# A factorization-machine layer on one core: P7's bank read in halves by two engines, a planner fed with traced durations, held-back loads and adding DMAs for X1, X2, X4

## The chip, the core and the metric

The kernel runs on one core of a Trainium2 chip. The metric is the device time in microseconds from launch to end, as the median of several runs. The profile used here is that of one execution.

The core has a matrix engine (PE; its weight loads are listed as PEld), a vector engine (DVE), a scalar engine (ACT), a general engine (POOL) and a queue engine that only starts DMAs (SP). ACT and POOL start DMAs too. PE writes its results into the banks of PSUM, 128 partitions of 512 fp32 values each; DVE and ACT read them there.

## The reference

```python
# x: (1024, 512), weight: (64, 512, 512) = (e, f, m), lin_w: (512, 512), lin_b: (512,)
out_lin = x @ lin_w.T + lin_b
xv = jnp.einsum('bf,efm->bem', x, weight)
zp = jnp.einsum('bf,efm->bem', jnp.square(x), jnp.square(weight))
interaction = 0.5 * jnp.sum(jnp.square(xv) - zp, axis=1)
return out_lin + interaction
```

All of it is fp32. The large part is `xv`: 1024 x 512 times 512 x 32768, squared and summed over the 64 embeddings. The sum over e of `zp` is one product of the squared x with the sum over e of the squared weights.

## The kernel before

**Products by Strassen's scheme.** Each product is cut into 2 x 2 quadrants and done with seven block products instead of eight (the variant of Winograd): P1 to P7 with left operands X1 to X7, which are quadrants or sums of quadrants of x, and right operands w11, w12, w21, w22 or T, which is a running sum of them. The columns of the weights come in 32 blocks (`h`, from 0 to 31), and each block runs the seven products in the order 5, 1, 6, 2, 3, 7, 4 (product 5 of the next block runs ahead of product 4 of this one). Each product has two halves of 256 batch rows, and each half uses one pair of PSUM banks, `bank_0` to `bank_3` in turn. A pair is one tile of shape [128, 2, 512]; `(bank, 0)` and `(bank, 1)` are its halves, one bank each.

**Operands in three pieces.** To use the fast fp32r matmul at fp32 accuracy, an operand is split into pieces H (rounded), L (the rest) and K (a small correction that pairs the two). `split` makes the pieces of a weight block: ACT copies H and a first L, then POOL, or an adding DMA issued by POOL (`dma_add`), completes L, and POOL makes K. `x_pieces` makes those of X1 to X7 once: ACT makes H, DVE makes L and K. A product half runs a "front" (H and L, 4 matmuls for each half of the pair), a scaling by DVE or ACT in place, and later a "back" (K, 2 matmuls for each half). In block 0 the products 1, 2 and 4 are plain fp32 matmuls without pieces (`PLAIN`).

**After a product.** For P2, P3, P4 and P7 `finish` lets ACT square the pair into `sq`, and DVE sums groups of 16 into `acc`. For P7 DVE also subtracts p5 from the pair, into `w`, which P4 of the same block adds. A pair can be written again, four halves later, when its readers are done: the pair of a half of P7 is next written by the same half of P4.

**Ends.** Ahead of the blocks stands the linear part, seven levels of plain fp32 matmuls (`one_level`, line 494 with `by_k`, line 507 without), whose operands R5, R6, R7, R3 and column sums `lt` are made by DVE, and whose results L11 to L22 go to DRAM. `f1` to `f4` are the four pairs there. Level 1 writes f1, ACT copies f1 to f2, level 2 adds into f1, and level 6 adds into f2. At the end the same scheme runs once more for `zp`, with the sums `acc` and the linear part added in.

**The order of the work** is written out ahead by a planner (`Plan`). Every operation is given with its engine's duration and what it reads and writes. PE's order is fixed by keys. From PE's order the planner works out for each operation the latest start (`deadlines`); then it plays the engines forward (`forward`), each taking the ready operation with the earliest latest start, repeats this 60 times with changed latest starts and keeps the order with the earliest end. `HOP` is the time from one engine's end to another's start, `AHEAD` how long before its latest start SP may issue a load. The planner fixes only the order on each engine; on the chip each instruction waits for its operands. DMA issues stand in the queue of the engine that issues them, and a waiting one holds back what is behind it.

Of the kernel before, what the change touches and what calls it, by code (L numbers as in the profile page):

```python
# [22 lines left out]

PLAIN = (1, 2, 4)
# [9 lines left out]
PE, DVE, ACT, POOL, SP = "PE", "DVE", "ACT", "POOL", "SP"  # L34
# [3 lines left out]
class Plan:  # L38
    HOP = 0.3
    OWN = 0.05  # L40
    AHEAD = 50.0
# [3 lines left out]
    YIELD = 0.0  # L45

# [27 lines left out]
    def deadlines(self, chain):  # L74
# [11 lines left out]
        while stack:  # L86
            o = stack.pop()
            latest = t if o.latest is None else o.latest
            cost = min(o.costs.values()) + o.move + o.land + self.HOP
# [50 lines left out]
    def forward(self, chain):  # L140
# [6 lines left out]
        done, late, nxt, wire, held = [], 0.0, 0, [9.0], None  # L147
# [5 lines left out]
        def ready(o, e=None):  # L153
            at = self.HOP
            for d in o.deps:
                own = ops[d].engine == e and not ops[d].move
                at = max(
                    at, ops[d].end + (self.OWN * (e != PE) if own else self.HOP * (e != NONE))
                )
            return at  # L160

        def ends(e, o, at):
            free[e], o.end, running[e] = at, at + o.land, o
# [3 lines left out]
            for t in (at, o.end, o.end + self.OWN, o.end + self.HOP):  # L167
# [7 lines left out]
        def pick(e, now):  # L175
# [23 lines left out]
        while len(done) < len(ops):  # L199
            now = heapq.heappop(times)  # L200
            moved = True
            while moved:
                moved = False
                for e in pending:
# [9 lines left out]
                    if e == PE:  # L214
                        nxt += 1
                        late = max(late, now - o.latest)
                    cost = o.costs[e]
                    o.start, o.engine = now, e
                    tensor = e == POOL and not o.move
                    if e == DVE and o.both and free[POOL] > now + 0.05 and not running[POOL].move:  # L220
                        held, free[e], o.end = o, float("inf"), float("inf")
                    elif tensor and held is not None and held.latest < o.latest + self.YIELD:
                        ends(DVE, held, now + held.costs[DVE])
                        o.after, held = held, None
                        ends(e, o, o.after.end + self.HOP + cost)
# [15 lines left out]
def kernel(  # L241
# [7 lines left out]
):  # L249

# [90 lines left out]
    def act(o, i, func, reads, writes, size=1024, scale=1.0, bias=0.0):  # L341
# [3 lines left out]
        plan.add({ACT: 0.14 + 0.92 * size / 1024}, emit, reads, writes)  # L345

    def stt(o, i, scalar, j, op, reads, writes, size=512, both=False, cost=None):
# [3 lines left out]
        plan.add({DVE: cost or 0.14 + 1.08 * size / 1024}, emit, reads, writes, both=both)  # L351

    def dve(o, a, b, sub, reads, writes, size=512, both=False):
# [3 lines left out]
        plan.add({DVE: 0.14 + 1.08 * size / 1024}, emit, reads, writes, both=both)  # L357

    def pool(o, a, b, sub, reads, writes, size=1024):
# [3 lines left out]
        plan.add({POOL: 0.15 + 2.35 * size / 1024}, emit, reads, writes)  # L363

    def reduce(o, i, reads, writes):
        plan.add(
            {DVE: 1.21},
# [6 lines left out]
    def dma(o, i, reads, writes, move=1.75, on=(SP,)):  # L374
        plan.add(dict.fromkeys(on, 0.45), lambda e: queues[e].dma_start(o, i), reads, writes,
                 land=2.0, move=move)

    def dma_add(o, i, reads, writes, move=2.75):
        plan.add(
            {POOL: 0.95}, lambda _: nc.gpsimd.dma_start(o, i, accum_op=ALU.add),  # L380
            tuple(reads) + tuple(writes), writes, land=2.5, move=move,
        )
# [20 lines left out]
    def load_x(n, k, lo, hi, at):  # L403
        r, q = quads[n]
        half = H // 2
        nc.sync.dma_start(
            buf[n][:, k, lo * half:hi * half],
            x_src[:, q * KH + k, r * H + lo * half:r * H + hi * half],
        )
        for u in range(lo, hi):  # L410
            landing((n, k, u), at)
# [9 lines left out]
    load_x("A11", 0, 0, 1, 3.5)  # L421
    load_lw(nc.scalar, [0], 0, 3.5)
    load_x("A11", 0, 1, 2, 3.9)
    load_lw(nc.scalar, [1], 0, 5.2)
    load_x("A11", 1, 0, 2, 5.0)
    load_lw(nc.scalar, [2, 3], 0, 7.2)
    load_x("A12", 0, 0, 2, 6.4)
    load_x("A12", 1, 0, 2, 7.4)
    load_lw(nc.sync, [0, 1], 1, 8.4)
    load_lw(nc.sync, [2, 3], 1, 9.2)  # L430
    for at, (n, k) in enumerate((("A22", 0), ("A22", 1), ("A21", 0), ("A21", 1))):
        load_x(n, k, 0, 2, 10.0 + 0.8 * at)
    nc.scalar.dma_start(bias[:], lin_b)
    landing("bias", 9.5)
    nc.scalar.preload_act_table(AF.Square)

    def a_parts(*names):
        return tuple((n, k, u) for n in names if n in quads for k in range(KH) for u in range(2)) + tuple(
# [46 lines left out]
    def one_level(p, rhs, left, bank, first, key, by_k=False):  # L485
# [3 lines left out]
        if by_k:  # L489
            for at, (u, k) in enumerate(steps):  # L490
                for half in range(2):
                    def emit(_, u=u, k=k, half=half):
                        cols = slice(half * H // 2, (half + 1) * H // 2)
                        nc.tensor.matmul(  # L494
                            buf[bank[u]][:, cols], b[:, k, ts(u, P)], a[:, k, cols],
                            start=first and k == 0 and half == 0, stop=k == KH - 1,
                            skip_group_check=True,
                        )

                    names = (a_names[2 * k + half],) + (b_names[k],)  # L500
                    plan.add({PE: WHOLE / 2}, emit, names + (bank[u],), (bank[u],),
                             key=key + 0.1 * at + 0.05 * half)
# [416 lines left out]
```

## Time and profile before

| | |
|---|---|
| Median of 3 runs | 1300.92 us (1297.79 to 1301.03) |
| Profiled execution: whole time | 1299.58 us |
| Profiled execution: span, first to last instruction | 1297.6 us |
| PE busy | 1280.1 us (99%) |
| DVE, ACT, POOL busy | 1086.7, 1011.9, 1095.3 us |
| Granted PE clock | 0.999 |
| DMA | 200.25 MB, mean 154 GB/s |

In the lines below, each instruction or group stands as line, engine, operation, output <- input, and shape. In a timeline the first number is the start and the second the duration in us, `x8` the number of records merged into the line, and in square brackets stands how long the engine had been idle before and what released it. A plain fp32 matmul has two records. In the list of groups the numbers after the bar are the busy time in us, the mean duration in ns, and the idle time just before, with its releasers. In the list of waits the numbers are us in total, times, and longest. In the list of DMAs the last number is the median time in us from issue to landing.

### The profile page before, as it was taken

To read this page: it belongs to the slowest core of one execution; us is meant where nothing else is said; L and a number is where in the kernel's file an instruction comes from. 1 tells how busy PE (TensorE), PEld (TensorE's weight loads), DVE (VectorE), ACT (ScalarE), POOL (GpSimd) and SP (SyncE) were. 2 spreads that over 40 slices of the span, in tenths; PEclk is the share of its full clock that TensorE was granted. 3 is DMA by queue.
4 is the path that set the end of the run, shared out by engine and by line. 5 is a ranking of instruction groups with operands and counts; after the bars stand their busy time and mean duration, and the time that the engine had idled before them with its cause. 6 is when DMAs were issued, how large, how long until landed. Compare 5 with 4: busy or idle time off the path is not lost.

```text
span 1297.6 us, 15705 instructions
## 1 busy us (share of the span) xinstructions
PE 1280.1 (99%) x5484; PEld 1026.0 (79%) x5484; DVE 1086.7 (84%) x954; ACT 1011.9 (78%) x1071; POOL 1095.3 (84%) x590
## 2 busy tenths in 40 slices
PE   8999999999999999999999999999999999999997
PEld 4668888888888888888888888888888888888873
DVE  4699888888888888888888888888888889888884
ACT  5568788788777888877888887788888788888872
POOL 3659898898888899889889888888988888998891
PEclk9999999999999999999999999999999999999999
DMA  6366676757667666677766666767667676766866
GB/s 226 97 164 160 155 170 150 158 129 154 163 155 167 142 152 145 149 163 164 162 147 143 153 151 161 167 145 161 133 148 168 147 162 152 169 131 144 184 130 150
DMA packets 75998, 200.25 MB, mean 154 GB/s; under 512 B 23824, under 2 KB 25104, under 8 KB 75920
## 3 DMA queue, kind: packets, MB, share of 16 engines
q0 software_dynamic: 28512, 101.72, 44.0%
q1 hardware_dynamic: 45552, 94.91, 22.6%
q10 hardware_dynamic: 1856, 2.62, 0.6%
q8 instruction: 43, 0.70, 0.2%
q14 instruction: 35, 0.29, 0.1%
HBM read 158.34 MB, written 6.29 MB: 127 GB/s over the span
## 4 chain that ended last, share of the span: by engine, by line
PE 92%; DMA 3%; DVE 2%; ACT 1%; issue 1%; POOL 1%; SPq 0%; DVEq 0%; ACTq 0%; POOLq 0%
PE bank L678 89%; PE bank L507 3%; DMA T<-weight 1%; DMA w<-weight 1%; DMA w<-xT 0%; PE bank L494 0%; DVE w L355 0%; POOL pL L361 0%; ACT sq L343 0%; ACT wsq L343 0%; POOL pK L361 0%; ACT pL L343 0%; DVE bank L355 0%; ACT bank L343 0%; DVE bank L349 0%
## 5 line engine op out<-in xcount | busy, mean ns | idle before, releaser
L361 POOL TENSOR_TENSOR pK<-pH,pL 128x1024 fp32r<-128x1024 f32 x221 | 560.1, 2554 | 19.8 <-PE bank L678 10.8
L343 ACT ACTIVATE sq<-bank 128x1024 f32<-128x1024 f32 x256 | 261.5, 1022 | 112.8 <-DVE w L355 52.2
L368 DVE TENSOR_REDUCE acc<-sq 128x16 f32<-128x1024 f32 x256 | 306.9, 1211 | 10.7 <-ACT sq L343 10.7
L361 POOL TENSOR_TENSOR pL<-w,pL 128x1024 fp32r<-128x1024 f32 x95 | 240.3, 2530 | 13.8 <-ACT pL L343 11.8
L361 POOL TENSOR_TENSOR pL<-T,pL 128x1024 fp32r<-128x1024 f32 x64 | 155.0, 2422 | 97.2 <-ACT pL L343 95.7
L349 DVE SCALAR_TENSOR_TENSOR bank<-bank,w 128x1024 f32<-128x1024 f32 x190 | 233.0, 1226 | 3.4 <-PE bank L678 3.4
L355 DVE TENSOR_TENSOR w<-bank,p 128x1024 f32<-128x1024 f32 x128 | 156.7, 1224 | 54.6 <-PE bank L678 52.4
L349 DVE SCALAR_TENSOR_TENSOR bank<-bank,p 128x1024 f32<-128x1024 f32 x126 | 154.4, 1226 | 44.9 <-ACT p L343 35.9
L343 ACT ACTIVATE pL<-T 128x1024 fp32r<-128x1024 f32 x95 | 100.9, 1062 | 83.5 <-issue 44.2
L343 ACT ACTIVATE pL<-w 128x1024 fp32r<-128x1024 f32 x126 | 133.8, 1063 | 36.0 <-issue 29.6
L368 DVE TENSOR_REDUCE w_sum<-wsq 128x16 f32<-128x1024 f32 x128 | 155.2, 1213 | 7.9 <-ACT wsq L343 7.2
L343 ACT ACTIVATE wsq<-w 128x1024 f32<-128x1024 f32 x128 | 134.7, 1052 | 2.7 <-DVE w_sum L368 2.6
L343 ACT ACTIVATE p<-bank 128x1024 f32<-128x1024 f32 x128 | 130.1, 1018 | 8.4 <-PE bank L678 6.9
L343 ACT ACTIVATE pH<-w 128x1024 fp32r<-128x1024 f32 x126 | 133.0, 1055 | 0.0
L712 DVE TENSOR_SCALAR bank<-bank 128x1024 f32<-128x1024 f32 x62 | 76.4, 1232 | 54.8 <-PE bank L678 54.7
L343 ACT ACTIVATE pH<-T 128x1024 fp32r<-128x1024 f32 x95 | 100.0, 1052 | 0.0
L380 POOL DMA_DIRECT2D T<-weight x93 | 99.4, 1069 | 0.0
L678 PE MATMUL bank<-pH,X3H 128*128 128x512 f32 x256 | 78.9, 389 | 1.0 <-DVE w L355 1.0
L678 PE MATMUL bank<-pH,X7H 128*128 128x512 f32 x256 | 79.2, 390 | 0.4 <-ACT sq L343 0.3
L678 PE MATMUL bank<-pH,X5H 128*128 128x512 f32 x256 | 79.4, 391 | 0.0
L678 PE MATMUL bank<-pH,X2H 128*128 128x512 f32 x248 | 76.5, 389 | 2.7 <-ACT pH L343 2.7
L678 PE MATMUL bank<-pL,X7L 128*128 128x512 f32 x256 | 78.9, 389 | 0.0
(116 smaller groups left out, 2550.1 us busy)
## 6 DMA issues: line engine op xcount, KB each, us to landing
w<-weight SPq DMA_DIRECT2D x128, 512.0 KB, 5.6
T<-weight POOLq DMA_DIRECT2D x93, 512.0 KB, 7.4
T<-weight SPq DMA_DIRECT2D x32, 512.0 KB, 3.6
pL<-T POOLq DMA_DIRECT2D x31, 512.0 KB, 6.1
pL<-w POOLq DMA_DIRECT2D x31, 512.0 KB, 5.2
w<-weight POOLq DMA_DIRECT2D x31, 512.0 KB, 5.3
accd<-turned SPq DMA_DIRECT2D x64, 32.0 KB, 5.0
p<-lind SPq DMA_DIRECT2D x4, 512.0 KB, 4.7
```

Source lines behind the costliest of these rows:

```text
L343: nc.scalar.activation(o, i, func, bias=bias, scale=scale)
L349: return nc.vector.scalar_tensor_tensor(o, i, scalar, j, ALU.mult, op)
L355: return (nc.vector.tensor_sub if sub else nc.vector.tensor_add)(o, a, b)
L361: return (nc.gpsimd.tensor_sub if sub else nc.gpsimd.tensor_add)(o, a, b)
L368: lambda _: nc.vector.tensor_reduce(o, i.rearrange("p a (m e) -> p a m e", e=E), axis=AX.X, op=ALU.add),
L380: {POOL: 0.95}, lambda _: nc.gpsimd.dma_start(o, i, accum_op=ALU.add),
L507: nc.tensor.matmul(buf[bank[u]], b[:, k, ts(u, P)], a[:, k, :], start=first and k == 0, stop=k == KH - 1, skip_group_check=True,)
L678: nc.tensor.matmul(buf[bank, j], buf[x][:, k, ts(2 * half + j, P)], buf[w][:, k, :], start=first and k == 0, stop=k == KH - 1, skip_group_ ...
L712: plan.add({DVE: 1.2}, lambda _, o=o: nc.vector.tensor_scalar(o, o, 1 + U, None, ALU.mult), names, names)
```

## The change

What it does, part by part:

- **P7's pair in halves.** ACT squares half 0 while DVE subtracts from half 1; then DVE takes half 0 and ACT half 1.
- **X1, X2, X4.** L and K are made by ACT copies and adding DMAs (two each) instead of by DVE.
- **Sums of weights in block 0** are adding DMAs from DRAM instead of POOL sums (`MORE`).
- **The linear part.** The first loads are 256 KB each, the weights' on ACT's queue, those of x on SP's. The first two levels use whole-width matmuls. Level 2 writes a pair of its own, DVE adds it to L11, and the copy f1 to f2 goes; level 6 adds into f1. The last part does the same: f1 is added to the output early, and two ACT copies go.
- **The planner** gets new durations, a tail for each engine, `HOP` 0.06, `AHEAD` 20, and `SOON`: POOL's DMAs are not issued more than 25 us before their latest start. A DMA that the planner held back gets a wait for the PE operation that was running then.
- The scale S moves from the pieces of X into the squares, and U into the reads of plain products. These cost no instruction.

The diff, cut to these parts:

```diff
+MORE = True
+X_SPLIT = {5: DVE, 6: DVE, 3: DVE, 7: DVE, 1: "DMA", 2: "DMA", 4: "DMA"}
+FIRST = dict.fromkeys(range(1, 8), "POOL")
...
-    HOP = 0.3
-    OWN = 0.05
-    AHEAD = 50.0
+    HOP = 0.06
+    TAIL = {"PE": 0.17, "DVE": 0.09, "ACT": 0.11, "POOL": 0.05, "SP": 0.0, "": 0.0}
+    AHEAD = 20.0
+    SOON = 25.0
...
+                if e == POOL and o.move and o.latest - self.SOON > now + 1e-6:
+                    heapq.heappush(times, o.latest - self.SOON)
+                    continue
...
+                    if o.move and o.emit and mark and now - ready(o, e) > 0.3 and now > free[e] + 0.1:
+                        o.after = mark
...
-        plan.add({ACT: 0.14 + 0.92 * size / 1024}, emit, reads, writes)
+        plan.add({ACT: 0.06 + 0.89 * size / 1024}, emit, reads, writes)
-        plan.add({DVE: 0.14 + 1.08 * size / 1024}, emit, reads, writes, both=both)
+        plan.add({DVE: 0.06 + 1.08 * size / 1024}, emit, reads, writes, both=both)
-        plan.add({POOL: 0.15 + 2.35 * size / 1024}, emit, reads, writes)
+        plan.add({POOL: 0.1 + 2.24 * size / 1024}, emit, reads, writes)
-    def dma_add(o, i, reads, writes, move=2.75):
+    def dma_add(o, i, reads, writes, move=3.1, land=1.8):
         plan.add(
-            {POOL: 0.95}, lambda _: nc.gpsimd.dma_start(o, i, accum_op=ALU.add),
+            {POOL: 0.62}, lambda _: nc.gpsimd.dma_start(o, i, accum_op=ALU.add),
...
-    load_x("A11", 0, 0, 1, 3.5)
-    load_lw(nc.scalar, [0], 0, 3.5)
-    load_x("A11", 0, 1, 2, 3.9)
-    load_lw(nc.scalar, [1], 0, 5.2)
-    load_x("A11", 1, 0, 2, 5.0)
-    load_lw(nc.scalar, [2, 3], 0, 7.2)
-    load_x("A12", 0, 0, 2, 6.4)
-    load_x("A12", 1, 0, 2, 7.4)
-    load_lw(nc.sync, [0, 1], 1, 8.4)
-    load_lw(nc.sync, [2, 3], 1, 9.2)
+    load_x("A11", 0, 3.9)
+    load_lw(nc.scalar, [0, 1], 0, 3.9)
+    load_x("A11", 1, 5.2)
+    load_lw(nc.scalar, [2, 3], 0, 5.6)
+    load_x("A12", 0, 7.4)
+    load_lw(nc.scalar, [0, 1], 1, 7.8)
+    load_x("A12", 1, 8.2)
+    load_lw(nc.scalar, [2, 3], 1, 8.8)
...
     def x_pieces(i):
         n, (h, l, k) = OPERAND[i], (f"X{i}{z}" for z in "HLK")
-        act(buf[h], buf[n], AF.Copy, a_parts(n), (h,), scale=S * TRIM)
-        stt(buf[l], buf[n], S, f32(h), ALU.subtract, a_parts(n) + (h,), (l,), 1024, True)
-        stt(buf[k], f32(h), -U, f32(l), ALU.add, (h, l), (k,), 1024, True)
+        parts = a_parts(n)
+        act(buf[h], buf[n], AF.Copy, parts, (h,), scale=TRIM)
+        if X_SPLIT[i] == "DMA":
+            act(buf[l], buf[n], AF.Copy, parts, (l,), scale=-TRIM)
+            dma_add(f32(l), buf[n], parts, (l,))
+            act(buf[k], buf[n], AF.Copy, parts, (k,), scale=-U * TRIM)
+            dma_add(f32(k), f32(l), (l,), (k,))
+        else:
+            dve(buf[l], buf[n], f32(h), True, parts + (h,), (l,), 1024, True)
+            stt(buf[k], f32(h), -U, f32(l), ALU.add, (h, l), (k,), 1024, True)
...
     one_level(1, lin_rhs, lhs, f1, True, -1000, True)
-    for u in range(2):
-        act(buf[f2[u]], buf[f1[u]], AF.Copy, (f1[u],), (f2[u],), 512)
-    one_level(2, lin_rhs, lhs, f1, False, -990, True)
     lin_copy("L11", f1, 0, 1.0)
+    one_level(2, lin_rhs, lhs, f2, True, -990, True)
+    lin_add("L11", f2, False)
     lin_store("L11", 0, 0)
...
-    one_level(6, lin_rhs, lhs, f2, False, -960)
+    one_level(6, lin_rhs, lhs, f1, False, -960)
...
-        if h:
+        if h or MORE:
             dma_add(buf[o], src(h, q), (), (o,))
...
     def finish(h, p, half, bank):
         row, col = {2: (0, 0), 3: (0, 1), 4: (1, 0), 7: (1, 1)}[p]
         sq, a = square(), acc_name[h // NCB]
-        act(buf[sq], buf[bank], AF.Square, both_of(bank), (sq,))
         m, b = (2 * col + h % NCB) * MI, row * NJ + 2 * half
+        if p == 7:
+            n, p5 = value["w", h, half], value["p5", h, half]
+            used((sq, 0), sq)
+            used((sq, 1), sq)
+
+            def square_of(k):
+                act(buf[sq][:, k], buf[bank, k], AF.Square, ((bank, k),), ((sq, k), (bank, k)),
+                    512, scale=S)
+
+            def rest_of(k):
+                dve(buf[n, k], buf[bank, k], buf[p5, k], True, (p5, (bank, k)),
+                    ((n, k), (bank, k)))
+
+            square_of(0)
+            rest_of(1)
+            rest_of(0)
+            square_of(1)
+            used(sq, (sq, 0), (sq, 1))
+        else:
+            act(buf[sq], buf[bank], AF.Square, both_of(bank), (sq,), scale=S)
         reduce(buf[a][:, b:b + 2, m:m + MI], buf[sq], (sq,), ((a, b // 2, m),))
...
-            if p == 7:
-                n, p5 = value["w", h, half], value["p5", h, half]
-                dve(buf[n], o, buf[p5], True, (p5, *names), (n,), 1024)
...
     one_level(1, right, left, f1, True, key)
     for u in range(2):
-        act(buf[f2[u]], buf[f1[u]], AF.Copy, (f1[u],), (f2[u],), 512, -1.0)
+        into(o_name[0, 0], f1, False, u)
...
-    one_level(2, right, left, f1, False, key + 20)
+    one_level(2, right, left, f2, True, key + 20)
```

More of the change, by code (lines that the diff above doesn't have):

```diff
@@ L22 @@
 TRIM = 1.0 - 2.0 ** -13
+PE, DVE, ACT, POOL, SP = "PE", "DVE", "ACT", "POOL", "SP"
 PLAIN = (1, 2, 4)
@@ L224, in forward @@
                         o.after, held = held, None
[L225 removed]
+                        ends(e, o, free[DVE] + 0.15 + cost)
                     elif tensor and held is None and free[DVE] > now and running[DVE].both:
@@ L490, in one_level, with emit @@
             for at, (u, k) in enumerate(steps):
[L491 to L502, printed above, removed]
+                def emit(_, u=u, k=k):
+                    return nc.tensor.matmul(
+                        buf[bank[u]], b[:, k, ts(u, P)], a[:, k, :], start=first and k == 0,
+                        stop=k == KH - 1, skip_group_check=True,
+                    )
+                plan.add({PE: WHOLE}, emit, (a_names[k], b_names[k], bank[u]), (bank[u],),
+                         key=key + 0.1 * at)
             return
@@ L885 @@
                 ),
-                reason="the port that VectorE and GpSimd share",
+                reason="the order of transfers, or of two engines at the port that they share",
             )
```

105 lines of the change are left out of this document (52 added, 53 removed).

## The prediction

> **What bounds the kernel now.** I read the profile's page first, then the busy time by stages, then who PE waited for, and last the timelines of the places where it waited.
>
> ```profile
> span 1297.6 us, 15705 instructions
> PE 1280.1 (99%) x5484; PEld 1026.0 (79%) x5484; DVE 1086.7 (84%) x954; ACT 1011.9 (78%) x1071; POOL 1095.3 (84%) x590
> ```
>
> PE is busy for 1280.1 of 1297.6 us, and the change keeps every matmul (32 half-width ones become 16 whole ones), so only the 17.5 us in which PE stands still can be won. The view by stages says where they lie; its first columns are the stretch, its length and PE's busy time in it.
>
> ```profile
> 0.00:33.10 33.10, 28.59 (x76) 14.91 (x77) 15.35 (x14) 18.09 (x23) 11.90 (x10) 1.00 0.68 222
> 33.10:95.00 61.90, 58.16 (x211) 39.21 (x210) 50.71 (x43) 37.46 (x39) 38.03 (x20) 1.00 0.46 130
> 95.00:150.00 55.00, 54.67 (x240) 44.40 (x239) 47.77 (x42) 42.37 (x46) 48.82 (x26) 1.00 0.67 152
> 150.00:1250.00 1100.00, 1099.88 (x4846) 905.93 (x4845) 943.55 (x824) 896.26 (x945) 978.12 (x521) 1.00 0.69 154
> 1250.00:1291.50 41.50, 38.76 (x118) 21.56 (x116) 26.86 (x30) 17.73 (x23) 18.48 (x16) 1.00 0.67 140
> 1291.50:1297.60 6.10, 0.01 (x1) 0.00 (x0) 2.49 (x4) 0.00 (x0) 0.00 (x0) 0.81 0.46 172
> ```
>
> Idle by stage: 4.51 us in the linear part, 3.74 in the first products, 0.33, then 0.12 in the 1100 us of the steady loop, 2.74 in the last level and 6.10 of adding and storing after the last matmul. The loop has nothing to give; it can only lose. The whole run of this profile took 1299.58 us, 1.98 more than its span and 1.34 below the median of 1300.92; I sum against 1299.58. About 0.3%, 3.9 us, is what can be told from no change: below 1297.0 is faster, above 1304.8 slower.
>
> **The linear part.**
>
> ```profile
> 4.33 2.25 PE L494 MATMUL bank<-w,p 128*128 128x256 f32 x8
> 8.18 1.53 PE L494 MATMUL bank<-w,p 128*128 128x256 f32 x6 [1.60 <-DMA w<-xT]
> 10.38 0.70 PE L494 MATMUL bank<-w,p 128*128 128x256 f32 x2 [0.67 <-ACT bank L343]
> 11.75 3.29 PE L494 MATMUL bank<-w,p 128*128 128x256 f32 x14 [0.67 <-ACT bank L343]
> 15.82 0.70 PE L494 MATMUL bank<-w,p 128*128 128x256 f32 x2 [0.78 <-ACT wsq L343]
> 16.36 3.60 PE L507 MATMUL bank<-w,p 128*128 128x512 f32 x8
> 19.79 7.03 PE L507 MATMUL bank<-sq,p 128*128 128x512 f32 x16
> 33.12 1.02 PE L678 MATMUL bank<-pH,X5H 128*128 128x512 f32 x2
> 9.75 0.58 ACT L343 ACTIVATE bank<-bank 128x512 f32<-128x512 f32 x1 [0.54 <-PE bank L494]
> 11.16 2.02 DVE L355 TENSOR_TENSOR p<-p,p 128x512 f32<-128x512 f32 x3
> w<-xT SPq DMA_DIRECT2D x5, 256.0 KB, 6.4
> p<-lin_wT ACTq DMA_DIRECT2D x2, 128.0 KB, 3.1
> ```
>
> The first two levels take from 4.33 to 16.36, 12.03 us. A level costs 3.43 (16.36 to 19.79), so 5.17 are lost: 1.60 to the second chunk of X, 0.67 twice to the copies of f1 into f2, 0.78 to the copy for L11, the rest to slow first matmuls and restarts. The change drops the two copies, puts the second level into another pair of banks, so that the reads for L11 hold back no matmul, and sends the X chunks with fewer transfers ahead of them. What it puts in their place: the first matmul needs 256 KB of each operand instead of 128 KB. 128 KB took 3.1 us to land, 256 KB 6.4 in the median, so that costs 0 to 3.3 us; I take 0.7, near the low end, because those 256 KB stood behind earlier transfers and these do not. The fourth level needs the column sums, which end at 11.16 + 2.02 = 13.18; it will be asked for at 4.33 + 0.7 + 6.86 = 11.9, so at most 1.3 is lost again. The weight halves that they need move to the front of ACT's queue; I take 0.4. With 0.7 of restarts, 1.8 of the 5.17 stays: gain 3.4, bounds 0.8 and 4.5.
>
> The next thing is late or not: the first product.
>
> ```profile
> L361 POOL TENSOR_TENSOR T<-T,w 128x1024 f32<-128x1024 f32 x3 | 8.0, 2659 | 17.8 <-DMA w<-weight 17.8
> L361 POOL TENSOR_TENSOR pL<-w,pL 128x1024 fp32r<-128x1024 f32 x95 | 240.3, 2530 | 13.8 <-ACT pL L343 11.8 <-DVE X6K L349 1.2
> L343 ACT ACTIVATE pL<-w 128x1024 fp32r<-128x1024 f32 x126 | 133.8, 1063 | 36.0 <-issue 29.6 <-PE bank L678 6.0 <-DMA w<-weight 0.3
> T<-weight POOLq DMA_DIRECT2D x93, 512.0 KB, 7.4
> ```
>
> POOL's first sum of T waited 17.8 us for its load and took 2.66. As an adding DMA it takes 7.4: landed by about 18 + 7.4 = 25.4, split by ACT (1.06) and POOL (2.53) at 29.0. PE asks at 33.12 - 3.4 = 29.7. It is covered by 0.7 us; if it lands later, the gain shrinks by as much.
>
> **The first products.**
>
> ```profile
> PE bank L678 <- ACT pH L343: 2.7, 1, 2.7
> PE bank L678 <- DVE w L355: 1.0, 1, 1.0
> SPq L375 <- ACT wsq L343: 672.8, 52, 28.5
> 82.40 1.22 DVE L349 SCALAR_TENSOR_TENSOR X2L<-w,X2H 128x1024 fp32r<-128x1024 f32 x1
> 83.64 8.98 DMA w<-weight
> L380 POOL DMA_DIRECT2D pL<-w x31 | 27.1, 875 | 9.0 <-ACT pL L343 8.4 <-ACT pH L343 0.6
> ```
>
> The large wait (2.7) is for a weight load that took 8.98 us on the chain of waits, and the loads came in a bunch because SP's queue had stood for up to 28.5 us behind one ACT square; the last of them waited for DVE to make X2L at 82.40. The 1.0 is DVE being late: in this stage it is busy for 50.71 of 61.90 us. The change takes six such DVE operations away (6 x 1.22 = 7.3 us) and adds six ACT copies (6 x 1.06 = 6.4; ACT is busy for 37.46 of 61.90, which hides them, and without that cover they would cost as much) and six POOL issues (6 x 0.88 = 5.3). Against these POOL loses four sums of 2.66 and issues four more DMAs in their place. DVE gains two adds of L11, about 1.3. The waits that the planner adds stand in front of DMAs: behind a waiting SP load stand SP's later loads and stores, behind a waiting POOL add stand POOL's pL and pK sums, for which PE waits. The planner lets POOL have a wait only where it was idle, so I cost these at nothing as long as POOL is idle a tenth of the time (978.12 busy of 1100). I take 2.9 of the 3.74 as gained; bounds +3.7 and -2.7, the last for one more stall of the size seen. From 95 to 150 us I take 0.2.
>
> **The last level.** Its waits are PE for DVE's and ACT's reads of a bank, and those reads stay: only the copies of f1 go, which no wait names, and two adds into the output come earlier on DVE. I take 0.4; bounds +1.2 and -0.8. The last 6.10 us stay.
>
> Together 3.4 + 2.9 + 0.2 + 0.4 = 6.9 us won.
>
> **P7 in halves.** This is the step that decides.
>
> ```profile
> 612.19 1.07 PE L678 MATMUL bank<-pK,X7K 128*128 128x512 f32 x4
> 613.30 1.22 DVE L355 TENSOR_TENSOR w<-bank,p 128x1024 f32<-128x1024 f32 x1 [0.37 <-PE bank L678]
> 614.61 1.03 ACT L343 ACTIVATE sq<-bank 128x1024 f32<-128x1024 f32 x1 [0.75 <-DVE w L355]
> 615.83 0.39 PE L678 MATMUL bank<-pH,X4H 128*128 128x512 f32 x1
> 147.26 0.73 PE L678 MATMUL bank<-pH,X7H 128*128 128x512 f32 x2 [0.33 <-ACT sq L343]
> 1281.86 0.68 DVE L355 TENSOR_TENSOR p<-p,bank 128x512 f32<-128x512 f32 x1
> 1282.45 0.69 DVE L355 TENSOR_TENSOR p<-p,w 128x512 f32<-128x512 f32 x1
> ```
>
> X7K ends at 613.26. DVE reads the pair of banks to 614.52, ACT waits for DVE and reads it to 615.64, and X4H writes the same pair at 615.83. So 2.57 us are there and 2.38 are used: PE misses a wait by less than 0.2 us. The change lets ACT square one half while DVE subtracts the other, and then they swap. If the halves are separate, the pair is free after about 0.04 + 0.68 + 0.68 + 0.04 = 1.44 us and nothing waits; that saves nothing either, since the loop has 0.12 us to give.
>
> But the traces say that a pair is not treated as two halves. Level 1 above has 8 + 6 + 2 = 16 records; its last two, at 10.38, write the second half of f1, and they waited for the ACT copy at 9.75, which reads the first half. The same holds at 15.82 against the copy for L11. So orders are kept between a read of one half and a write of the other; DVE and ACT, two readers, are already ordered on one pair (0.75 <- DVE w). If both hold, the four half reads go one after another: 0.04 to start, ACT 0.58, 0.03 across, DVE two halves 0.59 + 0.69 (1281.86 to 1282.45, and the second's length), 0.09 across, ACT 0.58, 0.04 to PE: 2.64 us against 2.57. X4H is 0.07 to 0.09 late, and a restart costs 0.73 - 0.62 = 0.11 more: 0.2 us. The second pair of the same product then has 0.2 more room and does not wait. There are 31 such products (32 weight blocks, less the first, whose product 4 is plain): 6.2 us lost.
>
> The Trainium skill (PSUM — Partial Sum Buffer, section "PSUM bank collisions raise a hardware error") states that two engines must not be in one bank and partition quadrant at once, reads against reads included, and that different banks run side by side. By that rule the two halves, which are two banks, could be read together, and the result would be the first rival's, not the sum with 6.2. The rows at 10.38 and 15.82 show an order stricter than that rule, for a read and a write; no row of this trace shows two readers on different halves.
>
> Sum: 1299.6 - 6.9 + 6.2 = 1298.9 us, no change that can be told.
>
> **The rivals.** First, the halves are read side by side: then 1299.6 - 6.9 = 1292.7. For it speaks that no row shows two readers of different halves ordered; against it the two rows above. Chance 0.27.
>
> Second, on the slow side: the halves go one after another and ACT comes late to the first. Before, ACT came free at 614.61 - 0.75 = 613.86, 0.56 us after DVE had begun; nobody felt it, as ACT was second. Now the first half is ACT's. Late by that much, every product costs 0.2 + 0.56 = 0.76 us, times 31 is 23.6: 1316.3. It makes the kernel slower from (1304.8 - 1292.7) / 31 = 0.39 us a product on. Against it: the planner now has the durations of the trace and can let ACT stand ready. Chance 0.15.
>
> Third, the loads held back come late in the first products, so that 2.9 gained become 2.7 lost: 1298.9 + 5.6 = 1304.5. Chance 0.08. The change not doing what it says is the forecast itself: P7's halves are then in turn by name only.
>
> **How the numbers follow.** Forecast 0.50, of which 0.17 lands below 1297.0 (the start and first products near their upper bounds, 1.1 + 0.8 more), 0.27 within, 0.06 above. First rival 0.27: 0.25 faster, 0.02 within. Second 0.15: 0.02 within, 0.13 slower. Third 0.08: 0.03 within, 0.05 slower. Together faster 0.42, within 0.34, slower 0.24. The range goes from 1289 (the first rival with every gain at its upper bound, 1292.7 - 1.1 - 0.8 - 0.8, and a little of the steady loop's restarts) to 1309 (half of the second rival's price); the forecast's own is 1295 to 1304.
>
> **What would show it.** Right: first product at 29 to 31 us, no wait over 1.5 us before 95, and in the loop X4H starting 2.6 to 2.8 us after X7K with ACT, DVE, DVE, ACT in a row and PE busy some 6 us less than 1100 between 150 and 1250. Wrong on P7: ACT and DVE halves of one product overlapping in time, and PE still at 1099.9. Wrong at the start: a wait of PE for pL of T, or for xT, of over 2 us.

## The result, and the profile after

The change makes the kernel much slower: 1399.22 us median (1395.73 to 1406.75), against 1300.35 us for the kernel before in the runs beside it, a ratio of 1.0775 (95% interval 1.0742 to 1.0808). The forecast was 1298.9 us with a range of 1289 to 1309. The profiled execution took 1405.92 us as a whole.

The page of after, its first lines, and then its busy time by stages (stretch, length, PE, PEld, DVE, ACT, POOL, clock, DMA share, GB/s):

```profile
span 1404.1 us, 15704 instructions
PE 1319.0 (94%) x5468; PEld 1025.4 (73%) x5468; DVE 1096.3 (78%) x1016; ACT 1025.2 (73%) x1137; POOL 1093.9 (78%) x596
```

```profile
0.00:33.10 33.10, 31.84 (x75) 14.92 (x76) 18.60 (x22) 24.41 (x28) 9.09 (x10) 1.00 0.82 251
33.10:95.00 61.90, 61.90 (x230) 42.98 (x229) 52.32 (x43) 41.86 (x45) 48.06 (x30) 1.00 0.84 193
...
150.00:1250.00 1100.00, 1033.53 (x4392) 823.52 (x4391) 867.01 (x798) 818.71 (x906) 885.05 (x473) 0.99 0.61 139
1250.00:1404.00 154.00, 137.61 (x542) 100.54 (x541) 112.46 (x113) 95.73 (x110) 105.44 (x62) 0.98 0.65 151
```

PE stands idle for 85.1 us (1404.1 - 1319.0), 67.6 more than before's 17.5, and it is busy for 38.9 us more with 16 records fewer. The first 95 us are better than before: idle there fell from 4.51 and 3.74 to 1.26 and 0.00. The loop, which had 0.12 us of idle time between 150 and 1250, has 66.47. All of the loss lies where the prediction said that nothing can be won.

Who PE waits for, in after (total us, times, longest):

```profile
PE bank L707 <- DMA pL<-T: 40.1, 23, 2.7
PE bank L707 <- ACT sq L354: 21.1, 58, 2.0
PE bank L707 <- DMA pL<-w: 12.0, 19, 1.7
```

None of these groups is of any size before, where the largest was a single wait of 2.7. The list counts only the standing still. If each record's start is compared with the start that an undisturbed row of matmuls would give, the records start 123.2 us late in total, 17.7 before; 47.8 of that lies ahead of X5L, 17.3 ahead of X3L, 37.1 ahead of X4H, and 8.6 in matmuls at a slower clock (last section). (X5L is the piece L of the left operand X5, and so on.) So after has two faults: operands by adding DMAs (`pL`) that come too late, and P7's pair, which comes free too late.

**The first fault**, in the timeline around 560 us of after and in its list of DMAs (last number: median us from issue to landing):

```profile
549.69 1.06 ACT L354 ACTIVATE pL<-T 128x1024 fp32r<-128x1024 f32 x1 [2.52 <-issue]
...
551.09 4.76 POOL L372 TENSOR_TENSOR pK<-pH,pL 128x1024 fp32r<-128x1024 f32 x2 [3.30 <-DMA pL<-w]
...
553.75 3.84 SPq L386 DMA_DIRECT2D w<-weight  x3
...
555.80 0.86 POOL L391 DMA_DIRECT2D pL<-T  x1
...
561.61 0.61 PE L707 MATMUL bank<-pH,X5H 128*128 128x512 f32 x2
564.23 0.74 PE L707 MATMUL bank<-pL,X5L 128*128 128x512 f32 x2 [2.01 <-DMA pL<-T]
```

```profile
pL<-T POOLq DMA_DIRECT2D x31, 512.0 KB, 8.0
pL<-w POOLq DMA_DIRECT2D x31, 512.0 KB, 9.2
```

ACT had the first L ready at 550.75. POOL issued the adding DMA only at 555.80: it had waited 3.30 us for the adding DMA before this one, and then made two K's up to 555.85. Meanwhile SP issued three weight loads between 553.75 and 557.59. PE asked at about 562.2 and got its operand at 564.23. Over the 31 blocks, for `pL<-T`, the median time from ACT's copy to the issue went from 0.3 us to 5.4, from the issue to the first use from 10.6 to 8.2, and the landing itself from 6.1 to 8.0 (`pL<-w`: 5.2 to 9.2). SP's weight loads issued between 4 us ahead of the add and 5 us behind it went from 1.1 to 2.9 on average. For `pL<-w` that count stayed at 0.9 and 1.0, so it doesn't explain why this landing grew; that stays open.

**The second fault**, in the same stretch: the four half reads of each of the two pairs of a product 7.

```profile
565.74 1.09 PE L707 MATMUL bank<-pK,X7K 128*128 128x512 f32 x4
566.87 0.69 DVE L366 TENSOR_TENSOR w<-bank,p 128x512 f32<-128x512 f32 x1 [2.70 <-PE bank L707]
567.65 0.60 ACT L354 ACTIVATE sq<-bank 128x512 f32<-128x512 f32 x1 [0.70 <-DVE w L366]
568.28 0.69 DVE L366 TENSOR_TENSOR w<-bank,p 128x512 f32<-128x512 f32 x1 [0.72 <-ACT sq L354]
568.49 1.07 PE L707 MATMUL bank<-pK,X7K 128*128 128x512 f32 x4
569.10 0.59 ACT L354 ACTIVATE sq<-bank 128x512 f32<-128x512 f32 x1
569.24 1.22 DVE L379 TENSOR_REDUCE w_sum<-wsq 128x16 f32<-128x1024 f32 x1 [0.26 <-ACT wsq L354]
569.74 0.73 PE L707 MATMUL bank<-pH,X4H 128*128 128x512 f32 x2 [0.19 <-ACT sq L354]
570.37 0.68 DVE L366 TENSOR_TENSOR w<-bank,p 128x512 f32<-128x512 f32 x1
571.15 0.60 ACT L354 ACTIVATE sq<-bank 128x512 f32<-128x512 f32 x1 [0.55 <-DVE w L366]
571.78 0.69 DVE L366 TENSOR_TENSOR w<-bank,p 128x512 f32<-128x512 f32 x1 [0.73 <-ACT sq L354]
572.59 0.59 ACT L354 ACTIVATE sq<-bank 128x512 f32<-128x512 f32 x1
573.23 0.73 PE L707 MATMUL bank<-pH,X4H 128*128 128x512 f32 x2 [0.47 <-ACT sq L354]
```

DVE, ACT, DVE, ACT: in these rows each starts when the other has ended, though the two halves are different banks. The first pair is written again 2.91 us after X7K's end (566.83 to 569.74), where 2.57 would not have been felt. The second is worse: X7K ends at 569.56, but DVE is in a sum of weights until 570.37, 0.81 us too long, and X4H starts 3.67 us after X7K. Of all 64 pairs, 60 show this order, and in these the last read ended 2.85 us or more after X7K (median 3.2). The second pairs of the products have the larger part of the 37.1 us ahead of X4H, 24.3.

### The profile page after: what moved, and what is told of

It reads as the page before. It is cut to its first block, busy times and chain, and to the rows that moved or that the text cites. A ratio compares the mean times of both kernels' runs of the same rounds, so it can differ in the third digit from the quotient of the medians.

```text
span 1404.1 us, 15704 instructions
## 1 busy us (share of the span) xinstructions
PE 1319.0 (94%) x5468; PEld 1025.4 (73%) x5468; DVE 1096.3 (78%) x1016; ACT 1025.2 (73%) x1137; POOL 1093.9 (78%) x596
## 5 line engine op out<-in xcount | busy, mean ns | idle before, releaser
L372 POOL TENSOR_TENSOR pK<-pH,pL 128x1024 fp32r<-128x1024 f32 x221 | 588.0, 2666 | 228.7 <-DMA pL<-T 128.0
L354 ACT ACTIVATE sq<-bank 128x1024 f32<-128x1024 f32 (+1 forms) x320 | 271.7, 850 | 137.7 <-issue 63.4
L372 POOL TENSOR_TENSOR pL<-w,pL 128x1024 fp32r<-128x1024 f32 x95 | 245.4, 2583 | 12.1 <-ACT pL L354 12.0
L366 DVE TENSOR_TENSOR w<-bank,p 128x512 f32<-128x512 f32 (+1 forms) x192 | 165.8, 865 | 113.1 <-PE bank L707 67.2
L372 POOL TENSOR_TENSOR pL<-T,pL 128x1024 fp32r<-128x1024 f32 x64 | 184.1, 2876 | 25.3 <-ACT pL L354 25.3
L707 PE MATMUL bank<-pL,X5L 128*128 128x512 f32 x256 | 85.1, 415 | 40.2 <-DMA pL<-T 40.1
L707 PE MATMUL bank<-pH,X4H 128*128 128x512 f32 x248 | 84.2, 421 | 21.1 <-ACT sq L354 21.1
L354 ACT ACTIVATE bank<-bank 128x1024 f32<-128x1024 f32 x64 | 65.1, 1017 | 47.6 <-PE bank L707 47.4
L707 PE MATMUL bank<-pL,X3L 128*128 128x512 f32 x256 | 81.4, 399 | 12.0 <-DMA pL<-w 12.0
L707 PEld LDWEIGHTS bank<-pL,X5L 128*128 128x128 f32 x256 | 47.7, 195 | 60.0 <-DMA pL<-T 51.1
```

The costliest lines, as they stand in the source:

```text
L354: nc.scalar.activation(o, i, func, bias=bias, scale=scale)
L366: return (nc.vector.tensor_sub if sub else nc.vector.tensor_add)(o, a, b)
L372: return (nc.gpsimd.tensor_sub if sub else nc.gpsimd.tensor_add)(o, a, b)
L707: made = nc.tensor.matmul(buf[bank, j], buf[x][:, k, ts(2 * half + j, P)], buf[w][:, k, :], start=first and k == 0, stop=k == KH - 1, skip ...
```

## The experiments

There were two questions: how much each fault costs by itself, and why the order of the plan became so bad. Each run is timed against the kernel before on the same chip, whose median in the three groups of runs was 1299.79 (`e1` to `e4`), 1298.38 (`e5` to `e8`) and 1300.35 (`e10` to `e13`); four runs each where nothing else is said. Every edit makes the planner write a new order, so a difference holds the whole new order and not only the operations named.

**P7's pair read whole again, the rest as in after** (`e1_p7_whole`).

```diff
-        if p == 7:
-            n, p5 = value["w", h, half], value["p5", h, half]
...
-            square_of(0)
-            rest_of(1)
-            rest_of(0)
-            square_of(1)
...
+        act(buf[sq], buf[bank], AF.Square, both_of(bank), (sq,), scale=S)
...
+            if p == 7:
+                n, p5 = value["w", h, half], value["p5", h, half]
+                dve(buf[n], o, buf[p5], True, (p5, *names), both_of(n), 1024)
```

> The changed kernel with P7's pair read whole again (ACT squares it, DVE subtracts from it), all else kept. Theory H (the four half reads go one after another and hold the pair 2.8 us where 2.57 are there): the waits before X4H, 37.1 us with their restarts, go, so about 1399 - 37 = 1362 us, and the waits for the adding DMAs of pL (65 us before X5L and X3L with restarts) stay. Rival (the late adding DMAs are the one cause and P7 only fills slack that they leave): PE meets the same DMAs later, X5L's waits grow by what X4H's lose, and the time stays above 1385.

1350.93 us, ratio 1.0400 (1.0381 to 1.0419). The halves cost about 48 us in this setting, but 51 stay. The list of waits of this run:

```profile
PE bank L688 <- DVE w L366: 31.4, 30, 1.1
PE bank L688 <- DMA pL<-T: 12.6, 21, 2.1
```

Here the plan took the two readers for parallel and often put ACT first, DVE late: 30 of the 60 pairs of P7 that X4H follows let PE wait for DVE. That flaw of the experiment is mended in `e5_p7_dve_first`.

**No holding back of loads** (`e2_no_hold`).

```diff
-    AHEAD = 20.0
+    AHEAD = 50.0
-    SOON = 25.0
+    SOON = 1000.0
-                    if o.move and o.emit and mark and now - ready(o, e) > 0.3 and now > free[e] + 0.1:
-                        o.after = mark
```

> The changed kernel without the holding back of transfers: AHEAD 50 and no SOON, and no wait of a DMA on a PE operation; P7 in halves as in the change. Theory L (held-back loads are let go in threes and run into the adding DMAs of pL, whose landing went from 6.1 to 8.0 and from 5.2 to 9.2 us): loads spread out again, X5L's and X3L's waits of 65 us and the 8.6 us of slow matmuls go mostly, 1320 to 1340 us, X4H's 37 stay. Rival D (the planner's short price for an adding DMA, 4.9 us where it was 5.25 and a HOP of 0.06 where it was 0.3, has them issued too late): the waits stay, 1380 to 1400.

**A longer price for the adding DMA, with the loads still held back** (`e3_land5`).

```diff
-    def dma_add(o, i, reads, writes, move=3.1, land=1.8):
+    def dma_add(o, i, reads, writes, move=3.1, land=5.0):
```

> The changed kernel with one number of the planner altered: an adding DMA is planned to land 5.0 us after its transfer instead of 1.8. Theory L: issued 3.2 us earlier the DMA still meets the bunched loads, but a lateness of 2 us is covered; 1340 to 1370. Rival D: the short price is the cause, and X5L's and X3L's waits go fully: 1325 to 1340. If neither is right the waits stay: 1390 or more.

1339.18 us (1.0307, 1.0292 to 1.0323) and 1325.42 us (1.0210, 1.0191 to 1.0228). The waits and the landing in the first, then in the second:

```profile
PE bank L705 <- POOL pL L370: 7.5, 2, 7.1
...
PE bank L705 <- ACT sq L352: 6.6, 32, 0.4
...
pL<-T POOLq DMA_DIRECT2D x31, 512.0 KB, 4.8
```

```profile
PE bank L707 <- ACT sq L354: 10.8, 29, 1.7
...
pL<-T POOLq DMA_DIRECT2D x31, 512.0 KB, 4.6
```

Either one takes away the waits for `pL` of T, by two ways; those for `pL<-w` shrink from 12.0 us to none named and to 1.8. Without holding back, fewer loads run beside the add (0.1 of SP's instead of 2.9) and it lands in 4.8 us. With the longer price it is issued 10.3 us ahead of its use instead of 8.2, and meets no load of SP either. By these two runs the first fault needs both: loads held back into a bunch, and an add issued too late to stand the bunch.

**The kernel before with P7's halves alone** (`e4_before_halves`): after's four half reads in place of the two whole ones.

> The kernel before with P7's pair read in halves and nothing else changed. Theory H: X4H waits in all 31 products, by 0.35 + 0.11 and 0.62 + 0.11 us as in the changed kernel: 1300 + 37 = 1337 us. What the prediction had: 0.2 us a product, 1306. Rival (halves read side by side when the plan is not tight): 1300.

1331.6 us, ratio 1.0251 (1.0235 to 1.0266). Its waits:

```profile
PE bank L699 <- ACT sq L343: 18.0, 32, 0.7
```

The halves by themselves cost 31.8 us, 1.06 a product (30 products: in the last block X4H starts before X7K ends and has nothing to wait for), nearly all of it ahead of X4H (31.5 us by the starts of the matmuls). Nothing else of the change is in this kernel. But most of it is not the fault seen in after. Here 41 of the 64 pairs are read in the forecast order ACT, DVE, DVE, ACT, and in 22 of the 60 that X4H writes again the last read comes behind X4H's own first matmuls:

```profile
349.17 0.60 ACT L343 ACTIVATE sq<-bank 128x512 f32<-128x512 f32 x1 [0.64 <-PE bank L699]
349.80 1.29 DVE L355 TENSOR_TENSOR w<-bank,p 128x512 f32<-128x512 f32 x2 [0.78 <-ACT sq L343]
...
351.69 0.61 PE L699 MATMUL bank<-pH,X4H 128*128 128x512 f32 x2
...
352.80 1.09 ACT L343 ACTIVATE sq<-bank 128x512 f32<-128x512 f32 x2 [1.14 <-PE bank L699]
353.45 0.73 PE L699 MATMUL bank<-pH,X4H 128*128 128x512 f32 x2 [0.69 <-ACT sq L343]
```

The planner takes the halves for separate, so it lets X4H write half 0 as soon as that is read. ACT's read of half 1 is then ordered behind these matmuls (1.14 us), and X4H's matmuls into half 1 wait for it (0.69). By the starts of the matmuls 21.1 of the 31.5 us lie ahead of these second writes. In after no pair is read so.

**After with the pair read whole, and DVE first in the plan** (`e5_p7_dve_first`), as in before; **the same with the longer price** (`e6_dve_first_land5`); **the same without holding back** (`e7_dve_first_land5_no_hold`).

```diff
+            if p == 7:
+                dve(buf[n], o, buf[p5], True, (p5, *names), both_of(n) + names, 1024)
...
-    def dma_add(o, i, reads, writes, move=3.1, land=1.8):
+    def dma_add(o, i, reads, writes, move=3.1, land=5.0):
...
-    AHEAD = 20.0
+    AHEAD = 50.0
-    SOON = 25.0
+    SOON = 1000.0
```

> The changed kernel with P7's pair read whole and in a planned order: DVE first, then ACT, so that the planner knows that they don't run together (before it fell out that way, 2.38 of the 2.57 us). Theory R (X4H's waits are readers of one pair that the planner takes for parallel, in halves or whole): the 39.6 us that e1 kept before X4H go: 1351 - 39.6 = 1311 us, with X5L's waits for the adding DMA left. Rival (the tight durations of the plan bring DVE late to the pair however it is read): X4H still waits 0.5 us or more a product, 1330 or more.

> As e5, and an adding DMA planned to land 5.0 us after its transfer. If P7's order and the price of the adding DMA are all that went wrong, what is left is the gain of the start: the first product at 29.5 instead of 33.1 us and 4 us of waits fewer up to 95, so 1300 - 8 = 1292 us (1288 to 1297). Rival (holding transfers back costs by itself, through bunched loads): X3L or X5L still wait, 1300 to 1315.

> As e6, without holding transfers back (AHEAD 50, no SOON, no waits of DMAs on PE). If holding back costs something beside the price, this is faster than e6 by 3 us or more; if it only mattered together with the short price, the two are the same within 3 us. It was e2's long single waits (up to 7.1 us, weights late in the first products) that speak for a third outcome: slower than e6 by 5 to 10, since early loads then crowd the first 100 us.

1331.09 (1.0256, 1.0204 to 1.0309), 1332.56 (1.0265, 1.0240 to 1.0290) and 1332.61 us (1.0262, 1.0247 to 1.0278). These are the misses of the study: P7's order is repaired in all three and the price in the last two, and yet some 33 us stay, in other places each time. In the first X4H still starts 17.3 us late in total, X5L 12.6 and X3L 6.4. In the second the waits for `pL` of T are gone (2.2 us stay for `pL<-w`) and X4H has 28.8. In the third X4H has 9.3, and there are single long waits, up to 8.0 us for a sum of POOL. In before the last read of the pair ends 2.39 us after X7K in the median and over 2.53 us after it in 4 of the 64 pairs; here that happens in about a third of them. What the three share, and before does not have, is the planner's new set of times.

**The kernel before with the holding back alone** (`e8_before_hold`).

```diff
-    AHEAD = 50.0
+    AHEAD = 20.0
+    SOON = 25.0
+                if e == POOL and o.move and o.latest - self.SOON > now + 1e-6:
+                    heapq.heappush(times, o.latest - self.SOON)
+                    continue
...
+                    if o.move and o.emit and mark and now - ready(o, e) > 0.3 and now > free[e] + 0.1:
+                        o.after = mark
```

> The kernel before with the holding back of transfers alone (AHEAD 20, SOON 25, waits on PE), old durations, P7 as before. Theory L (held loads bunch and lengthen the landing of pL's adding DMAs): their landing rises from 6.1 and 5.2 to 8 us or more and X5L waits, 1315 to 1350 us. Rival D (the old price, 0.95 + 2.75 + 2.5 + 0.3, issues them 10.6 us before use, which covers 8 to 9 us): 1300 within 4.

1297.27 us, ratio 0.9991 (0.9982 to 1.0000), ten runs. Holding back by itself costs nothing here; the wait of 2.7 us in the first products is gone (PE is busy for 60.90 of the 61.90 us from 33.10 to 95.00, 58.16 before). So the expectation that held-back loads hurt by themselves fell. The add lands in 6.0 us here, with 1.9 loads of SP beside it, but it is issued 10.6 us ahead of its use.

**`e5` with the planner's old times** (`e10_old_times`): everything of the change but the halves, the durations, `HOP` and the tails. **`e5` with the old `HOP` and no tails, the new durations kept** (`e11_hop_alone`).

```diff
-    HOP = 0.06
-    TAIL = {"PE": 0.17, "DVE": 0.09, "ACT": 0.11, "POOL": 0.05, "SP": 0.0, "": 0.0}
+    HOP = 0.3
+    TAIL = {"PE": 0.0, "DVE": 0.0, "ACT": 0.0, "POOL": 0.0, "SP": 0.0, "": 0.0}
+                elif ops[d].engine == e and not ops[d].move:
+                    at = max(at, ops[d].end + 0.05)
...
-        plan.add({ACT: 0.06 + 0.89 * size / 1024}, emit, reads, writes)
+        plan.add({ACT: 0.14 + 0.92 * size / 1024}, emit, reads, writes)
...
-    def dma_add(o, i, reads, writes, move=3.1, land=1.8):
+    def dma_add(o, i, reads, writes, move=2.75, land=2.5):
...
-            {POOL: 0.62}, lambda _: nc.gpsimd.dma_start(o, i, accum_op=ALU.add),
+            {POOL: 0.95}, lambda _: nc.gpsimd.dma_start(o, i, accum_op=ALU.add),
```

The lines from the first `plan.add` on stand in the first kernel alone, and there the durations of DVE, POOL and the plain DMAs go back in the same way.

> As e5 (the changed kernel, P7's pair whole, DVE before ACT) with the planner's old, longer durations, its HOP of 0.3 and no tails; start, adding DMAs, held-back transfers stay as changed. Theory M (the durations of the trace leave the plan no margin, so that DVE and ACT come late to P7's pair in a third of the products, 2.7 to 4.1 us where 2.57 are there, and pL's DMAs are issued late): the pair is free at 2.39 us again, X4H, X5L and X3L don't wait, and the gain of the start shows: 1288 to 1296 us. Rival (the new mix of operations, more ACT copies and DMAs, is what makes engines late): X4H still waits, 1310 or more.

> As e5 with HOP 0.3 and no tails alone, the short durations kept. If the step from engine to engine carries the margin: 1290 to 1300, as e10. If the durations of the operations carry it: as e5, 1320 to 1335.

1298.77 us (0.9988, 0.9977 to 0.9998; ten runs) and 1309.91 us (1.0074, 1.0055 to 1.0092). The waits of the first:

```profile
PE bank L690 <- ACT p L356: 3.4, 3, 2.5
PE bank L690 <- DMA pL<-w: 1.5, 2, 1.2
```

With the old times the 32.7 us of `e5` are gone, and P7's pair is free at 2.39 us again. Of the 34 us between `e5` and `e10`, set against the kernel before each time, the step from engine to engine carries 23 us (`e5` to `e11`; the runs of `e5` spread by 14.7 us, so this is rough) and the durations 11 (`e11` to `e10`). The first product starts at 28.71 here, so the start is gained as in after; 3.4 us of new waits for ACT's copies out of a pair and 1.5 for `pL` take part of it back.

**The kernel before with the new times alone** (`e12_before_new_times`), the counterpart of `e10`, and **after with the old times, its halves kept** (`e13_halves_old_times`). The edits are those above, the other way round in the first.

> The kernel before with the planner's new durations, HOP 0.06 and tails, and nothing else. Theory M: the loss appears here without P7's halves, without held-back transfers and without new DMAs: late readers at P7's pair and late DMAs of pL, 1325 to 1360 us. Rival (the loss needs the new operations): 1300 within 5.

> The changed kernel with P7's halves kept and the planner's old durations, HOP 0.3 and no tails. This is the cost of the halves by themselves in the new kernel: the four reads in a row take at least 2.64 us of 2.57. By the prediction's 0.2 us a product 6 us over e10; by what e4 showed beside the kernel before (31.8 us) 30 us over e10.

1357.9 us (1.0452, 1.0427 to 1.0478) and 1336.27 us (1.0273, 1.0252 to 1.0293). The new times alone cost the kernel before 57.6 us, more than any other part. A second pair of product 7 in `e12`:

```profile
596.71 1.07 PE L678 MATMUL bank<-pK,X7K 128*128 128x512 f32 x4
...
597.48 1.22 DVE L368 TENSOR_REDUCE acc<-sq 128x16 f32<-128x1024 f32 x1 [1.16 <-ACT sq L343]
...
598.62 1.21 DVE L355 TENSOR_TENSOR w<-bank,p 128x1024 f32<-128x1024 f32 x1
...
599.92 1.03 ACT L343 ACTIVATE sq<-bank 128x1024 f32<-128x1024 f32 x1 [1.56 <-DVE w L355]
...
601.00 0.73 PE L678 MATMUL bank<-pH,X4H 128*128 128x512 f32 x2 [0.50 <-ACT sq L343]
```

DVE stood idle for 1.16 us for ACT's square, then summed it, and so read P7's pair 0.84 us after X7K's end at 597.78. The order on DVE is fixed ahead with this sum in front of the read, so the read can't pass it. In this run X4H starts over 2.65 us after X7K in 30 of 60 pairs, in before in one. In the other kernel the halves cost 37.5 us on top of `e10` (1336.27 - 1298.77), of which 25.0 lie ahead of X4H. Taken out of after, the new times are worth about as much as they cost the kernel before: 63 us (98.9 for after less 35.9 for `e13`, each over the kernel before).

So the parts stand as follows, each by itself against the kernel before: the new times +57.6, the halves +31.8 (+37.5 beside the other parts), all the rest -1.6. Their sum is 87.8 or 93.5, the change as a whole 98.9. The rest of 5 to 11 us was not taken apart. The -1.6 has an interval from -3.0 to -0.3 us and can hardly be told from nothing. That the sum comes so near is at least in part luck, for the places do not add up: `e4` loses two thirds of its time in a way that after doesn't show, and `e12` loses ahead of X4H, X2H and X1H (24.3, 14.5, 9.8) and hardly waits for `pL`, which is issued 10.7 us ahead of its use there and lands in 4.6.

A rival is that any new order would be worse than the one of before. The runs speak against it: the orders written with the old times and the pair whole (before, `e8`, `e10`) lie between 1297 and 1301 us, those with the new times (`e1`, `e5`, `e6`, `e7`, `e12`) between 1331 and 1358, and `e11`, with half of the old times, at 1310.

## Why the prediction was wrong, point by point

**The planner's new times: the step that failed by most.** The prediction had no term for them in its sum. It costed the held-back waits at nothing, and in the second rival it took the durations of the trace as help: "the planner now has the durations of the trace and can let ACT stand ready". `e12` shows +57.6 us for them alone, `e10` that the rest of the change without them and without the halves is 1.6 us faster than before. The old values were longer than the trace's: 0.3 us from engine to engine, where the rows show 0.04 to 0.19, and 1.22 us of DVE, where operations in a row start 1.14 us apart (597.48 and 598.62 above). That this was the margin that let DVE and ACT stand ready at P7's pair, where 2.38 of 2.57 us are used, is read from such rows and from `e11`; no run changes the margin alone. The prediction had both numbers and stated that PE misses a wait by less than 0.2 us; what it did not ask was which allowance kept every one of those reads on time.

**Held-back loads.** "Nothing" was right by itself (`e8`) and wrong in combination: together with the short price of the adding DMA its landing got longer (6.1 to 8.0 us) and its lead shorter (10.6 to 8.2). The third rival put this into the first products at 5.6 us; it came in the loop, where PE waited 52.1 us for the two `pL` (40.1 + 12.0), and did not come in the first products at all. The sum's term for it was 0; the records ahead of X5L and X3L start 65 us late.

**P7 in halves.** The mechanism was right: the four reads go one after another, and a pair is not treated as two halves. By the Trainium skill (PSUM — Partial Sum Buffer, section "PSUM bank collisions raise a hardware error") different banks may be read side by side; the trace agrees for banks of different pairs: from 558.65 us DVE scales one pair for 1.22 us, and from 559.08 ACT squares another. For the two halves of one pair it shows nothing of the hardware, since each read waited for the one ahead by the program's own order (0.70 and 0.72 us in the rows above). The first rival, which needed them side by side, is out. The term was mis-sized: 0.2 us a product was computed, 1.06 measured in `e4`, 1.24 in after (37.1 over 30; the prediction counted 31 products, but in the last block X4H doesn't follow X7K). The chain as computed was good: in `e2`, where half of the pairs have the forecast order, its four reads take 2.54 us, 2.56 by the prediction's sum. What was wrong for after is the order, DVE, ACT, DVE, ACT, with three crossings between the engines instead of two (2.82 us); the start, which in half of the pairs is some 0.8 us late because the reading engine is busy; and the second pair, which should not have waited and has most of the loss. In `e4` a fourth thing is added: X4H's writes into one half and ACT's read of the other take turns. The rows at 10.38 and 15.82 had shown this order, and the sum used it for the reads alone. The second rival had the second of these, with a price of 0.76 a product and 1316.3 us; it was the nearest of the four cases, but had ACT as the late engine, where DVE was. The upper end of the range, 1309, was not quite what it was said to be: half of the 17.4 us that this rival adds to the forecast gives 1307.6.

**The start and the first products.** Right. The first product started at 29.45, inside 29 to 31, no matmul from 33.1 to 95 waited, and the copies of f1 no longer stand between the levels. In the timeline of after:

```profile
5.02 7.83 PE L504 MATMUL bank<-w,p 128*128 128x512 f32 x16 [0.48 <-DMA p<-lin_wT]
12.69 3.60 PE L515 MATMUL bank<-w,p 128*128 128x512 f32 x8
...
29.45 1.02 PE L707 MATMUL bank<-pH,X5H 128*128 128x512 f32 x2
```

The first two levels take from 5.02 to 12.69, 7.67 us instead of 12.03; the first matmul comes 0.69 us later, near the 0.7 that was chosen from 0 to 3.3. The first product is 3.67 us earlier (33.12 to 29.45); together with 3.74 us in the first products this is 7.4 us, against 6.3 forecast for the two. `e8` has 2.7 of these 3.74 by holding loads back alone, so little of it is left for the DVE operations that were taken away. The 0.4 us of the last level did not come: from the last product to the last matmul it is 19.74 us, 19.72 before, and what follows took 7.1 us instead of 6.1.

**The last step.** "The loop has nothing to give; it can only lose" was right, and it was priced by one wait only. An order that leaves 0.12 us of idle time in 1100 is what every changed planner constant writes anew, and the sum treated it as unchanged.

## What to carry to other kernels

If a fixed order is made from durations, the durations are not only estimates but the margins of that order. Replacing them by the medians of a trace takes margin out of every place at once, and here it showed where the slack was smallest (0.19 us). That deserves a term of its own, and a run of the old kernel with the new durations alone (`e12`) measures it. It is not bounded by the slack: a reader that is late by a whole operation costs as much (0.84 us in the rows of `e12`). Splitting a tile between two readers can gain only if the program orders the halves apart, for the writes as well as the reads, so look first for a pair of instructions on different halves that overlap in the trace.

## What was not expected of the hardware

After some waits of about 2 us the matmuls ran at nearly half speed for a while. In the timeline of after, and in its view by stages (stretch, length, busy time of PE, PEld, DVE, ACT and POOL, granted clock, DMA share, GB/s):

```profile
520.92 0.72 PE L707 MATMUL bank<-pL,X5L 128*128 128x512 f32 x2 [2.12 <-DMA pL<-T]
...
522.01 1.06 PE L707 MATMUL bank<-pL,X5L 128*128 128x512 f32 x2
522.86 1.91 PE L707 MATMUL bank<-pK,X7K 128*128 128x512 f32 x4
```

```profile
518.47:521.88 3.41, 1.29 (x6) 0.83 (x5) 1.84 (x2) 1.98 (x3) 0.87 (x1) 1.00 0.73 279
521.88:525.29 3.41, 3.41 (x10) 2.66 (x9) 0.48 (x1) 1.01 (x1) 3.41 (x3) 0.50 0.19 24
559.43:562.84 3.41, 2.79 (x13) 1.98 (x11) 2.80 (x3) 2.58 (x4) 0.00 (x0) 1.00 1.04 279
562.84:566.25 3.41, 2.02 (x9) 1.65 (x10) 1.22 (x1) 1.33 (x3) 1.93 (x1) 1.00 0.50 191
```

From 521.88 to 525.29 the trace records a granted clock of 0.5, and from 522.0 on the starts are 0.43 us apart instead of 0.23. This adds 8.6 us in after, over 43 records; the mean granted clock is 0.991 against 0.999 before. There are six such stretches in the loop of after, each 3.41 us long, and they begin a whole number of 3.41 us apart. If the trace is cut into windows of this length on the same grid, each of the six follows a window in which PE stood idle for 1.89 to 2.51 us, and no window at full clock with 1.82 us or less is followed by one. In the first window above PE was idle for 2.12 us. The wait of 2.01 us that ended at 564.23 was followed by nothing: the grid cut it at 562.84 into 0.62 and 1.39 us. Over all 14 traces the border is nearly as sharp (one stretch in `e3` follows 1.76 us). The Trainium skill (TensorE: Matmul & The Clock Gate, Part 1) gives half the clock after an idle window of about 3.4 us; here 1.89 of 3.41 us were enough, and so a wait of 2 us in a full loop can cost 1.4 us more than its own length (8.6 us over six).
